# A graph attention layer: scores moved into PSUM, messages, queries and copies reordered

## The chip, the cores and the metric

The kernel runs on one core of one Trainium2 chip. The metric is device time in microseconds (us) of one execution. Five engines work from their own instruction queues: TensorE (PE; its weight loads are shown apart as PEld), VectorE (DVE), ScalarE (ACT), GpSimd (POOL) and SyncE (SP, which here only issues DMAs). An engine runs its instructions in program order, and semaphores order the engines among each other. So an instruction that waits holds up everything queued behind it on its engine. Line numbers (L630) are those of the kernel before; the profile shows one execution.

## The reference

One layer of a graph network: 6250 nodes with 64 channels, 4 heads of 16 channels, and 206250 directed edges sorted by their destination (each node has a loop on itself).

```python
Qh = (x @ Wq.T + bq).reshape(n, H, D)
Kh = (x @ Wk.T + bk).reshape(n, H, D)
Vh = (x @ Wv.T + bv).reshape(n, H, D)
Ee = (edge_attr @ We.T + be).reshape(-1, H, D)
score = (Kh[src] * Qh[dst] * (1.0 / np.sqrt(D)) * Ee).sum(-1)
score = jnp.exp(jnp.clip(score, -5.0, 5.0))
msg = Vh[src] * score[..., None]
wV = jax.ops.segment_sum(msg, dst, num_segments=n)
return layernorm(x + wV.reshape(n, H * D))
```

## The kernel before

A first stage (154 us, up to the first L600) computes k and v of every node into a table in HBM (`kv_tab`), the queries into another (`q3_tab`), and splits x into three bf16 parts (`parts`) that stay in SBUF. The rest is the loop over edges.

**Tiling.** The edges make 1612 tiles of 128 (an edge per partition). 8 tiles are a *group* (`g`, 202 of them), and an iteration of the main loop (L703) bears a group's number. Two groups are a *step* (`s`; the last 8 steps have one group). Four groups, two steps, are called a *round* here (`m = g // 4`, `i = g % 4` is the place in it).

**k and v of the sources.** They go into one of KVB = 5 buffers per step, a row per edge, in two ways. For 14 of the 16 tiles of a step GpSimd issues one indirect DMA per tile (`gather_kv`, L446; `gather(s)` issues a whole step's: first the 8 of the even group, then 6 of the odd one). A buffer is read by the messages of its step, so its refill waits for these: the 8 for the even group's message, the 6 for the odd group's. The other two tiles of a step are computed in 47 rounds, for the four tiles of two steps at a time. Their x rows are picked out of `parts` by products with one-hot matrices: VectorE compares (`hots`, L503, 13 a round in 7 buffers), TensorE multiplies (`picks`, L514 into bank `pick` and L519 into bank `low`, 100 matmuls a round). ScalarE copies the result into x2 and x1 (L526, L527). TensorE then multiplies by the k and v weights (`picked_kv`, a bias product at L530 and four products at L533 and L535, into `rooms`), and ScalarE copies the rows into the buffer (`place_kv`, L541).

**A group.** Its work, from iteration to iteration:

- `edges` (L435): the edge products, 8 fp32 matmuls into a `pe` bank (there are two, by turns), on top of a bias that ScalarE wrote there (`biases`, L564).
- `onehot_rows` (L571) and `onehot_rows_rest` (L577), ScalarE: a one-hot matrix `to` for each tile, which picks the row of each destination out of a window `qw` of 42 rows of the query table. `queries` (L594): 8 matmuls of `to` by `qw` into a `pq` bank (two, by turns), one iteration before each is used at the latest.
- `products` (VectorE): k times query (L600), times edge product (L601), sum over the 16 channels of a head (L604), clamp (L606).
- `weigh` (L610, ScalarE): the exponential, in place. `message` (L617, VectorE): v times the exponential into `msg`.
- per step: `onehot_edges` (L585, VectorE) and `widen` (L625, ScalarE) make a one-hot matrix of destinations, `sums` (L630, TensorE, 16 matmuls) adds the messages of equal destinations into `pa`, and `add` (L644, VectorE, two instructions) puts `pa` into the ring `acc`.
- when a block of 128 nodes is complete: `close`, `spreads`, `roots`, `scales`, `norm` (L658 to L683), the layer norm.

**Shared banks.** `pa` and `rooms` are two parts of one PSUM bank, `room`. Every reader and writer of one part is ordered against those of the other as the program stands: `picked_kv` behind the `add` that precedes it, `place_kv` behind the `sums` of its iteration, the next `add` behind `place_kv`.

**The order within an iteration** (L703 to L777) is written by hand, and each engine takes its own part of it. For iteration g before the change:

- VectorE: products(g), one hot, add of the step that ended at g-3, message(g-1), for odd g onehot_edges, the other hots of g+1, closes and norms.
- TensorE: picks of g, edges(g+1), for odd g-2 sums, queries(g+2), for even g picked_kv. (At i = 0 the picks come last.)
- ScalarE: the copies into x2 and x1 at i = 0, onehot_rows(g+4) and its rest, sources (the picks' comparands), widen, place_kv, biases(g+2), weigh(g).
- GpSimd: at the first group of step s, gather(s+4), whose 8 first DMAs wait for the message of the even group of step s-1 and whose 6 last for that of its odd group.
- SP: fetches of edge attributes, windows and keys, some groups ahead.

The `hots` of iteration g are compares for the picks of g+1. A hot waits until the picks (the low ones last) of the hot seven before it are done.

Of the kernel before, what the change touches and what calls it, by code (L numbers as in the profile page):

```python
# [7 lines left out]
F32 = mybir.dt.float32  # L8
# [6 lines left out]
P = 128  # L15
N = 6250
C = 64
H = 4
# [3 lines left out]
G = 8  # L22
NG = -(-T // G)

STEPS = [(g, 2) for g in range(0, NG - 8, 2)] + [(g, 1) for g in range(NG - 8, NG)]
NS = len(STEPS)
# [12 lines left out]
KVB = 5  # L39
# [9 lines left out]
def tiles_of(g):  # L49
    return min(G, T - g * G)  # L50


def tiles_in(s):
    return sum(tiles_of(g) for g in groups_of(s))


def groups_of(s):
    return range(STEPS[s][0], STEPS[s][0] + STEPS[s][1])
# [6 lines left out]
LAST = (NS - 8 - AHEAD) // 2  # L65
# [15 lines left out]
def is_picked(g, j):  # L81

    s = max(s for s in range(NS) if STEPS[s][0] <= g)
    return picks_in(s - AHEAD) and g == groups_of(s)[-1] and j >= G - 2
# [23 lines left out]
def tile_gnn(ctx: ExitStack, tc: tile.TileContext, x, xT, wT, bias, beT, weT, eT, src, src_rows, dst,  # L108
# [335 lines left out]
    def gather_kv(g, j):  # L444
        t = g * G + j
        nc.gpsimd.indirect_dma_start(  # L446
            out=kv_of(g)[:, j, :], out_offset=None, in_=kv_tab[:, :],
            in_offset=bass.IndirectOffsetOnAxis(ap=src_i[:, t:t + 1], axis=0))
# [8 lines left out]
    with tc.If(rv == 0) as branch:  # L457

        with tc.tile_pool(name="work", bufs=2) as work, \
# [3 lines left out]
            TO, OH, OF, PE, PQ, MSG, KB, SCORE, HOT, FROM, SRC = ({} for _ in range(11))  # L463
# [16 lines left out]
            def pairs(ap):  # L480

                return ap.rearrange("p (a b) -> p a b", b=2)
# [7 lines left out]
            def sources(m):  # L490
                if m < LAST:
                    FROM[m] = work.tile([P, BATCH * P], BF16, name="from")
                    nc.scalar.activation(FROM[m], SRC.pop(m), AF.Identity, bias=minus_row50)
# [5 lines left out]
            def hots(m, c):  # L499
                lo, hi = CUTS[c], CUTS[c + 1]  # L500
                HOT[m, c] = work.tile([P, MOST, BATCH * P], BF16, name="hot", bufs=7)
                shape = [P, hi - lo, BATCH * P // 2, 2]
                nc.vector.tensor_tensor(  # L503
                    HOT[m, c][:, :hi - lo].rearrange("p b (a c) -> p b a c", c=2),
                    pairs(FROM[m])[:, None].to_broadcast(shape),
                    block2[:, lo:hi, None, :].to_broadcast(shape), op=OP.is_equal)
# [31 lines left out]
            def place_kv(m, i):  # L538
                to = 2 * m + AHEAD + i
                n = tiles_in(to)  # L540
                nc.scalar.activation(kvs[to % KVB][:, n - 2:n, :], rooms, AF.Copy)  # L541

            def gather(s):

                for g in groups_of(s):
                    for j in range(tiles_of(g)):
                        if not is_picked(g, j):
                            gather_kv(g, j)
# [13 lines left out]
            def biases(g):  # L562
                n = tiles_of(g)
                nc.scalar.activation(pe_all[g % 2][:, :n, :],  # L564
                                     be_all[:, None, :].to_broadcast([P, n, C]), AF.Copy)
# [24 lines left out]
            def queries(g):  # L590
                PQ[g] = pq_all[g % 2]
                n = tiles_of(g)
                for j in range(n):
                    nc.tensor.matmul(PQ[g][:, j, :], TO[g][:, j, :], QW[g], start=j == 0,  # L594
                                     stop=j == n - 1, skip_group_check=True)

            def products(g):
                n = tiles_of(g)
                prod = work.tile([P, G, C], F32, name="prod")
                nc.vector.tensor_mul(prod[:, :n, :], kv_of(g)[:, :n, :C], PQ[g][:, :n, :])  # L600
                nc.vector.tensor_mul(prod[:, :n, :], prod[:, :n, :], PE[g][:, :n, :])  # L601
                SCORE[g] = work.tile([P, G, H], F32, name="score", bufs=3)
                score = SCORE[g][:, :n]
                nc.vector.tensor_reduce(score, prod[:, :n, :].rearrange("p g (h d) -> p g h d", h=H),  # L604
                                        axis=AX.X, op=OP.add)
                nc.vector.tensor_scalar(score, score, -5.0, 5.0, op0=OP.max, op1=OP.min)  # L606
# [5 lines left out]
            def message(g):  # L612
                s, k = place_of(g)
                if k == 0:
                    MSG[s] = work.tile([P, 2 * G, C], F32, name="msg")
                n = tiles_of(g)
                nc.vector.tensor_mul(MSG[s][:, k:k + n, :].rearrange("p g (h d) -> p g h d", h=H),  # L617
                                     kv_of(g)[:, :n, C:].rearrange("p g (h d) -> p g h d", h=H),
                                     SCORE[g][:, :n, :, None].to_broadcast([P, n, H, D]))

            def widen(s):

                n = tiles_in(s)
                OF[s] = work.tile([P, 2 * G, P], F32, name="off", bufs=1)
                nc.scalar.activation(OF[s][:, :n, :], OH.pop(s)[:, :n, :], AF.Copy)  # L625
# [61 lines left out]
            step_of = {g: s for s in range(NS) for g in groups_of(s)}  # L687
            ends = {groups_of(s)[-1]: s for s in range(NS)}
# [11 lines left out]
                queries(g)  # L700
            for mc in pieces(0):
                hots(*mc)
            for g in range(NG + 1):  # L703
                now, before = g < NG, g > 0
                i, m = g % 4, g // 4
                todo, ahead = pieces(g), pieces(g + 1)
                if g % LG == 0 and g + 2 * LG < NG:
                    fetch_edges(g // LG + 2)
                if i == 0 and m:
                    fetch_sources(m + 1)  # L710
                if g + 4 < NG:
                    fetch_queries(g + 4)
                if g + 6 < NG:
                    fetch_keys(g + 6)
                done = ends.get(g - 3)
                if now:
                    products(g)
                for mc in ahead[:1]:
                    hots(*mc)
                if done is not None:  # L720
                    add(done)
                if i == 0 and 0 < m <= LAST:
                    picked(m - 1)
                if i:
                    picks(todo)
                if 2 <= g + 1 < NG:
                    edges(g + 1)
                if g - 2 in ends:
                    sums(ends[g - 2])
                if g + 2 < NG:  # L730
                    queries(g + 2)
                if i in (0, 2) and 4 <= g <= 4 * LAST + 2:
                    picked_kv(i // 2)
                if i == 0:
                    picks(todo)
                if g + 4 < NG:
                    onehot_rows(g + 4)
                    onehot_rows_rest(g + 4)
                if i == 2 and g < 4 * LAST:
                    sources(m + 1)  # L740
                if g - 1 in ends:
                    widen(ends[g - 1])
                if i in (1, 3) and 4 <= g <= 4 * LAST + 3:
                    place_kv(m - 1, i // 2)
                if g + 2 < NG:
                    biases(g + 2)
                if now:
                    weigh(g)
                else:
                    add(NS - 2)  # L750
                if before:
                    message(g - 1)
                if now and g == groups_of(step_of[g])[0] and step_of[g] + KVB - 1 < NS:
                    gather(step_of[g] + KVB - 1)
                if g in ends:
                    s = ends[g]
                    t0 = STEPS[s][0] * G
                    for t in range(t0, t0 + tiles_in(s)):
                        if t and t % KEYS == 0:
                            keys(t)  # L760
                    onehot_edges(s)
                for mc in ahead[1:]:
                    hots(*mc)
                if done is not None:

                    while closed < B - 2 and due[closed] <= done + 1:
                        close(closed)
                        spreads(closed)
                        closed += 1
                    if closed in BATCHES and closed > scaled:  # L770
                        roots(scaled, closed)
                        scales(scaled, closed)
                        scaled = closed
                    for _ in range(3):
                        if normed < scaled:
                            norm(normed)
                            normed += 1  # L777
# [182 lines left out]
```

## Time and profile before

| | |
|---|---|
| runs | 2503.68, 2481.4, 2481.17 us |
| median of these | 2481.4 us |
| the profiled execution's own time | 2496.53 us |
| its span, first to last instruction | 2494.6 us |
| mean granted TensorE clock | 0.825 |
| TensorE busy (12299 matmuls) | 1935.9 us, 78% |
| TensorE weight loads | 1331.1 us, 53% |
| VectorE busy | 1494.2 us, 60% |
| GpSimd busy | 1350.8 us, 54% |
| ScalarE busy | 908.6 us, 36% |
| DMA, mean over the span | 92 GB/s |

All durations in the text come from the profiled execution. In a row of the profile's groups, the first pair of numbers is the busy time of all the group's instructions (us) and the mean of one (ns); behind the next bar stand the idle time of the engine just before them and what ended most of it. "issue" is time in which the engine waited for nothing that the profile shows, "remote" a release whose instruction it can't name. In the timeline a row is the start (us), the duration, the engine, line and instruction, "xN" for N in a row, and in brackets the idle time before it. In the windows a row is a stretch, its length, and the busy time of each engine in it with the number of its instructions; then the clock that TensorE was granted (1.00 is full), the share of time that the DMA engines were busy, and what they moved.

The first L600 starts at 154.0 us and the last at 2473.1; between them lie some 50 rounds; all 40 slices of the page between start and end look alike (TensorE busy 70 to 80%, clock 0.7 to 0.8), so the time is a matter of the round.

### The profile page before, as it was taken

The page shows a single profiled execution, that of the slowest core. Times are in us where ns is not written, and L with a number is a line of the kernel's source. Part 1 is how long each engine was busy: PE and PEld are TensorE (multiplying, and loading weights), DVE is VectorE, ACT ScalarE, POOL GpSimd, SP SyncE. Part 2 cuts the span into 40 slices and gives each one's busy share as a digit, 9 for nine tenths or more (in the row PEclk, how much of TensorE's full clock was granted, in tenths as well). Part 3 has the DMA queues.
Part 4 walks back from the last instruction along what each step waited for, and adds up shares of the span by engine and source line. Part 5 has one row for each costly group of instructions (what it writes and reads, how often), then busy time and mean ns, then how long its engine had stood idle before and what let it go on. Part 6 is the DMA issues. An engine that isn't in the chain of part 4 may idle for free. (4 is left out here: it accounts for less than half of the span.)

```text
span 2494.6 us, 32642 instructions
## 1 busy us (share of the span) xinstructions
PE 1935.9 (78%) x12299; PEld 1331.1 (53%) x12299; DVE 1494.2 (60%) x2314; ACT 908.6 (36%) x1268; POOL 1350.8 (54%) x1434
## 2 busy tenths in 40 slices
PE   4477887887887887877778788788788778788875
PEld 4435555555555555455555555555555555455574
DVE  2356665665666666666556566566666666666653
ACT  1242433433442434233424234233343343342452
POOL 5435555555555555555555555555555555555551
PEclk9978888887887888788788788788888788888865
DMA  4332333333332333333323233233333332332341
GB/s 119 125 96 77 100 91 86 99 97 82 99 97 80 98 91 104 87 83 97 95 82 92 79 101 98 78 99 90 91 103 86 88 101 79 95 93 83 87 114 25
DMA packets 140877, 228.84 MB, mean 92 GB/s; under 512 B 71126, under 2 KB 71576, under 8 KB 140598
## 3 DMA queue, kind: packets, MB, share of 16 engines
q1 hardware_dynamic: 94758, 133.30, 18.3%
q0 software_dynamic: 45568, 92.37, 14.2%
q8 instruction: 98, 1.61, 0.3%
q10 hardware_dynamic: 384, 1.00, 0.2%
q14 instruction: 69, 0.57, 0.1%
HBM read 218.74 MB, written 7.79 MB: 91 GB/s over the span
## 5 line engine op out<-in xcount | busy, mean ns | idle before, releaser
L446 POOL DMA_INDIRECT kv<-kv_tab,src_i x1392 | 1319.3, 948 | 1086.1 <-DVE msg L617 642.3
L503 DVE TENSOR_TENSOR hot<-from,still 128x2048 bf16<-128x2048 bf16 (+1 forms) x611 | 697.2, 1173 | 156.9 <-PE low L519 117.0
L630 PE MATMUL room<-msg,off 128*128 128x64 f32 x3224 | 498.3, 298 | 284.8 <-issue 277.4
L630 PEld LDWEIGHTS room<-msg,off 128*128 128x128 f32 x3224 | 472.9, 220 | 304.3 <-issue 296.0
L514 PE MATMUL pick<-hot,parts 128*128 128x512 bf16 x2350 | 583.8, 401 | 9.3 <-issue 9.0
L541 ACT ACTIVATE kv<-room 128x256 f32<-128x256 f32 x94 | 36.2, 385 | 1379.0 <-PE room L630 511.8
L514 PEld LDWEIGHTS <-parts 128*128 128x128 bf16 x2350 | 235.7, 103 | 299.1 <-issue 88.7
L601 DVE TENSOR_TENSOR prod<-prod,pe 128x512 f32<-128x512 f32 x202 | 138.8, 687 | 418.4 <-remote 323.7
L435 PE MATMUL pe<-we_sb,et 128*128 128x128 f32 x1612 | 292.0, 331 | 110.5 <-ACT pe L564 68.9
L435 PEld LDWEIGHTS pe<-we_sb,et 128*128 128x128 f32 x1612 | 243.3, 229 | 182.7 <-ACT pe L564 88.9
L519 PE MATMUL low<-hot,parts 128*64 128x512 bf16 x2350 | 306.1, 386 | 14.5 <-issue 13.8
L577 ACT ACTIVATE to<-to,one_p 126x1024 bf16<-126x1024 bf16 x202 | 232.0, 1148 | 6.6
L571 ACT ACTIVATE to<-kb,minus_row 126x1024 bf16<-126x1024 bf16 x202 | 230.0, 1139 | 10.9 <-remote 5.5
L519 PEld LDWEIGHTS <-parts 128*64 128x64 bf16 x2350 | 120.3, 110 | 190.0 <-issue 114.8
L625 ACT ACTIVATE off<-of 128x2048 f32<-128x2048 bf16 (+2 forms) x105 | 191.9, 1828 | 52.5 <-remote 20.8
L644 DVE SCALAR_TENSOR_TENSOR acc<-room,above,acc 128x64 f32<-128x64 f32 x103 | 29.0, 282 | 243.2 <-ACT kv L541 177.9
L600 DVE TENSOR_TENSOR prod<-kv,pq 128x512 f32<-128x512 f32 x202 | 137.5, 681 | 25.2 <-remote 6.8
L594 PE MATMUL pq<-qw,to 126*128 126x64 bf16 x1612 | 109.7, 217 | 50.4 <-issue 40.2
L617 DVE TENSOR_TENSOR msg<-kv,score 128x512 f32<-128x512 f32 x202 | 138.7, 687 | 16.9 <-ACT score L610 12.7
L604 DVE TENSOR_REDUCE score<-prod 128x32 f32<-128x512 f32 x202 | 138.3, 685 | 6.9
L594 PEld LDWEIGHTS <-to 126*128 126x128 bf16 x1612 | 103.4, 120 | 61.1 <-issue 56.5
L585 DVE TENSOR_TENSOR of<-still,key 128x2048 bf16<-128x2048 bf16 (+2 forms) x105 | 123.3, 1175 | 0.2
(122 smaller groups left out, 1050.1 us busy)
## 6 DMA issues: line engine op xcount, KB each, us to landing
et<-in_eT SPq DMA_DIRECT2D x100, 512.0 KB
kb<-key_tab SPq DMA_DIRECT2D x201, 252.0 KB
kv<-kv_tab,src_i POOLq DMA_INDIRECT x1392
srcs<-in_src_rows SPq DMA_DIRECT2D x47, 256.0 KB
qw<-q_tab SPq DMA_DIRECT2D x202, 15.8 KB
kv_tab<-kv_sb SPq DMA_DIRECT2D x5, 640.0 KB
q_tab<-q SPq DMA_DIRECT2D x5, 480.0 KB
acc<-in_x SPq DMA_DIRECT2D x48, 32.0 KB
```

The source lines that it names most:

```text
L435: nc.tensor.matmul(pe[:, 2 * u:2 * u + 2, :], et[:, u, :], we_sb, start=False, stop=u == n // 2 - 1, skip_group_check=True)
L446: nc.gpsimd.indirect_dma_start(out=kv_of(g)[:, j, :], out_offset=None, in_=kv_tab[:, :], in_offset=bass.IndirectOffsetOnAxis(ap=src_i[:, t ...
L503: nc.vector.tensor_tensor(HOT[m, c][:, :hi - lo].rearrange("p b (a c) -> p b a c", c=2), pairs(FROM[m])[:, None].to_broadcast(shape), bloc ...
L514: nc.tensor.matmul(hi_mid, parts_flat[:, at:at + 2 * C], hot, start=b == 0, stop=b == NB - 1)
L519: nc.tensor.matmul(low[u * C:(u + 1) * C], parts_flat[:, at:at + C], hot, start=b < 2, stop=b >= NB - 2, skip_group_check=True)
L571: nc.scalar.activation(TO[g][:, :n, :], KB.pop(g)[:, :n * P].rearrange("p (j e) -> p j e", j=n), AF.Square, bias=minus_row3[:3 * W])
L577: nc.scalar.activation(TO[g][:, :n, :], TO[g][:, :n, :], AF.Relu, bias=one_p[:3 * W], scale=-1.0)
L594: nc.tensor.matmul(PQ[g][:, j, :], TO[g][:, j, :], QW[g], start=j == 0, stop=j == n - 1, skip_group_check=True)
L601: nc.vector.tensor_mul(prod[:, :n, :], prod[:, :n, :], PE[g][:, :n, :])
L617: nc.vector.tensor_mul(MSG[s][:, k:k + n, :].rearrange("p g (h d) -> p g h d", h=H), kv_of(g)[:, :n, C:].rearrange("p g (h d) -> p g h d", ...
L625: nc.scalar.activation(OF[s][:, :n, :], OH.pop(s)[:, :n, :], AF.Copy)
L630: nc.tensor.matmul(pa, OF[s][:, j, :], MSG[s][:, j, :], start=j == 0, stop=j == n - 1)
```

## The change

Four edits in the kernel's loop.

- **Scores.** `SCORE[g]` is no longer a tile of its own in SBUF, but the first 32 floats of the group's own `pq` bank (the queries, which L601 has not read, but L600 has, by the time L604 writes). L604, L606, L610 and L617 then work on PSUM, and the next queries into that bank, those of g+2, come behind the message of g.
- **Message.** message(g) stands at the end of iteration g, behind onehot_edges and the hots; it was in iteration g+1, behind the first hot and the add.
- **Queries.** Iteration g issues queries(g+1); it was queries(g+2). The first two are issued ahead of the loop as before.
- **ScalarE.** The order is now onehot_rows, weigh, biases, widen, sources, place_kv.

And the gathers: with KVB = 5, gather(4) is issued ahead of the loop, and gather(s+5) at the end of step s, behind its last message; it was gather(s+4) at the first group of step s. The order of the gathers and what each waits for are unchanged.

```diff
@@ products
-                SCORE[g] = work.tile([P, G, H], F32, name="score", bufs=3)
+                SCORE[g] = PQ[g][:, 0, :G * H].rearrange("p (g h) -> p g h", h=H)
@@ before the loop
+            gather(KVB - 1)
             for g in range(NG + 1):
@@ in the loop
                     edges(g + 1)
                 if g - 2 in ends:
                     sums(ends[g - 2])
-                if g + 2 < NG:
-                    queries(g + 2)
+                if 2 <= g + 1 < NG:
+                    queries(g + 1)
                 if i in (0, 2) and 4 <= g <= 4 * LAST + 2:
                     picked_kv(i // 2)
...
                 if g + 4 < NG:
                     onehot_rows(g + 4)
                     onehot_rows_rest(g + 4)
-                if i == 2 and g < 4 * LAST:
-                    sources(m + 1)
-                if g - 1 in ends:
-                    widen(ends[g - 1])
-                if i in (1, 3) and 4 <= g <= 4 * LAST + 3:
-                    place_kv(m - 1, i // 2)
-                if g + 2 < NG:
-                    biases(g + 2)
                 if now:
                     weigh(g)
                 else:
                     add(NS - 2)
-                if before:
-                    message(g - 1)
-                if now and g == groups_of(step_of[g])[0] and step_of[g] + KVB - 1 < NS:
-                    gather(step_of[g] + KVB - 1)
+                if g + 2 < NG:
+                    biases(g + 2)
+                if g - 1 in ends:
+                    widen(ends[g - 1])
+                if i == 2 and g < 4 * LAST:
+                    sources(m + 1)
+                if i in (1, 3) and 4 <= g <= 4 * LAST + 3:
+                    place_kv(m - 1, i // 2)
                 if g in ends:
...
                     onehot_edges(s)
                 for mc in ahead[1:]:
                     hots(*mc)
+                if now:
+                    message(g)
+                if g in ends and ends[g] + KVB < NS:
+                    gather(ends[g] + KVB)
                 if done is not None:
```

More of the change, by code (lines that the diff above doesn't have):

```diff
@@ L702, in tile_gnn @@
                 hots(*mc)
+            gather(KVB - 1)
             for g in range(NG + 1):
-                now, before = g < NG, g > 0
+                now = g < NG
                 i, m = g % 4, g // 4
```

## The prediction

> **What bounds the kernel now.** I read the page first: engine table, slices, chain, groups. TensorE is the busiest engine (78%), but its idle time is not spread evenly, and the chain of waits names only the last microseconds. So the groups come next, for what ends idle time:
>
> ```profile
> L446 POOL DMA_INDIRECT kv<-kv_tab,src_i x1392 | 1319.3, 948 | 1086.1 <-DVE msg L617 642.3
> L630 PE MATMUL room<-msg,off 128*128 128x64 f32 x3224 | 498.3, 298 | 284.8 <-issue 277.4
> L541 ACT ACTIVATE kv<-room 128x256 f32<-128x256 f32 x94 | 36.2, 385 | 1379.0 <-PE room L630 511.8
> L601 DVE TENSOR_TENSOR prod<-prod,pe 128x512 f32<-128x512 f32 x202 | 138.8, 687 | 418.4 <-remote 323.7
> L435 PE MATMUL pe<-we_sb,et 128*128 128x128 f32 x1612 | 292.0, 331 | 110.5 <-ACT pe L564 68.9
> L644 DVE SCALAR_TENSOR_TENSOR acc<-room,above,acc 128x64 f32<-128x64 f32 x103 | 29.0, 282 | 243.2 <-ACT kv L541 177.9
> ```
>
> Two readings. The sums (L630) lose 285 us to "issue", waiting for nobody. And VectorE's L601 waits 324 us for a release that the profile cannot name. Third, the timeline of one half of a round of four groups (a round lasts 46.4 us on average, 47 of them pick rows):
>
> ```profile
> 928.53 0.62 PE L519 MATMUL low<-hot,parts 128*64 128x512 bf16 x4 [0.34 <-issue]
> 928.57 0.39 ACT L541 ACTIVATE kv<-room 128x256 f32<-128x256 f32 x1 [15.12 <-remote]
> 928.99 0.28 DVE L644 SCALAR_TENSOR_TENSOR acc<-room,above,acc 128x64 f32<-128x64 f32 x1 [5.16 <-ACT kv L541]
> 929.62 0.69 DVE L617 TENSOR_TENSOR msg<-kv,score 128x512 f32<-128x512 f32 x1 [0.16 <-ACT score L610]
> 930.58 0.94 POOL L446 DMA_INDIRECT kv<-kv_tab,src_i  x1 [3.63 <-DVE msg L617]
> 930.83 0.28 PE L530 MATMUL room<-bkv_p,ones_b 3*128 3x256 bf16 x1
> 936.13 1.16 PE L435 MATMUL pe<-we_sb,et 128*128 128x128 f32 x8
> 937.12 1.51 PE L630 MATMUL room<-msg,off 128*128 128x64 f32 x12
> 939.14 0.32 PE L630 MATMUL room<-msg,off 128*128 128x64 f32 x1 [0.51 <-issue]
> 946.84 0.94 POOL L446 DMA_INDIRECT kv<-kv_tab,src_i  x1 [0.30 <-issue]
> 950.39 1.75 PE L630 MATMUL room<-msg,off 128*128 128x64 f32 x7 [0.44 <-issue]
> 950.46 0.69 DVE L601 TENSOR_TENSOR prod<-prod,pe 128x512 f32<-128x512 f32 x1 [8.30 <-remote]
> ```
>
> L601 at 950.46 needs the edge products L435, which ended at 937.3: TensorE's signal reached VectorE 13 us late. Meanwhile TensorE issued about one matmul per 0.7 us. Both end 2.6 us after GpSimd finished a run of 14 gathers, one each 1.25 us (930.58 to 947.78). Counted over the trace, gathers under 0.6 us apart form 53 runs of 8, 48 of 6 and 45 of 14. In all three lengths TensorE's signals, good up to about 3 us into a run, mostly wait for its end: the first one after it comes 1.3, 1.6 and 2.6 us later (medians). Of 428 us that TensorE idles between 180 and 2330 us, 317 lie between 8 us after the start of a run of 14 and 2.7 us after its end; 6's and 8's have 91 in all. That is an inference from timing, not a mechanism I can see. The windows of the same stretch:
>
> ```profile
> core 0: us, PE busy (x) PEld busy (x) DVE busy (x) ACT busy (x) POOL busy (x), PEclk, DMA share, GB/s
> 930.60:939.00 8.40, 8.03 (x62) 5.23 (x59) 8.04 (x13) 6.43 (x8) 6.57 (x7) 1.00 0.69 182
> 939.00:950.40 11.40, 3.92 (x14) 3.12 (x14) 3.15 (x4) 0.00 (x0) 6.65 (x8) 0.61 0.17 46
> ```
>
> TensorE goes from 8.03 busy of 8.40 to 3.92 of 11.40, and its granted clock falls to 0.61, while DMA is nearly idle: no bandwidth limit. (The Trainium skill, "TensorE: Matmul & The Clock Gate", HAM clock gate, says an idle window of about 3.4 us halves the clock; the clock column agrees, and by that rule the waits of 1.3 and 2.0 us priced below would not add half-clock time of their own.)
>
> So: TensorE paces a round, and each gather run both blocks its signals and, if long, starves it. What matters of the change is which TensorE signals VectorE needs when, and how messages (which release gathers) cluster.
>
> **The change, part by part.**
>
> *Scores in the PSUM bank.* Same instructions. L600 reads one PSUM operand (681 ns), L601 too (687), L617 none (687): under 10 ns for PSUM, so 0, with ±0.01 x 3 x 202 = 6 us. (The Trainium skill, "Perfetto Trace Analysis", Identifying Performance Opportunities, gives VectorE about 60 ns of access overhead on SBUF, 125 on PSUM. By that, an estimate, 65 ns x 3 x 202 = 39 us if nothing hides it; no row here shows it, and VectorE idles 40%.) What the bank costs is order: queries of g+2 now wait for the message of g.
>
> *Queries one iteration later.* The same 8 weight loads and matmuls per group, now of g+1. Products of g+1 follow at once, so VectorE loses its lead: today it waits at L601 for the edge products, ahead of the sums; now at L600 for the queries, which follow the sums. ScalarE's one-hot rows also wait for the later queries, still 2.3 us ahead of the exponential's need. Put in times: an even iteration will start with the signal of the queries, which stand right behind the sums on TensorE. Where both were held back and land together, that is when L541 starts today (928.57, plus 0.1); where the sums ended by themselves (the first group of a round), the queries end 0.4 after L541 starts (904.33 + 0.64 = 904.97 against 904.57). Then products 2.35 (L600 0.79, L601 to the next hots 1.54), hots 1.2, and both adds 0.5 plus a gap: done 4.2 us after. The bias product of the picked rows (L530) needs these adds (they read the same bank). Today it starts 930.83 - 928.57 = 2.3 us after L541 in the third group of a round and 907.93 - 904.57 = 3.4 in the first. It will be 4.3 and 4.7: +2.0 and +1.3, 3.3 us of TensorE per round, 47 x 3.3 = **+155**. Lower bound 0: TensorE would have idled anyway in the following run. Upper bound: none of it hidden, which is what I take, as L530's successors wait behind it in order. What was queued behind on TensorE: all picks of the next group.
>
> *Copies of picked rows last on ScalarE.* Removes the wait of biases (L564) and exponential behind L541, hence of L435 for L564: 68.9 us + 3.8 for L625. This gain is already inside the +1.3 and +2.0, because today's 3.4 contains it. Widening is behind the exponential now: 1.9 us, done some 5 us after the products, while the next sums are a group away: 0; without that cover, 1.9 per step. The adds of the next even group wait for L541 as before.
>
> *Message in its own iteration, gathers after it.* Queue behind a waiting message on VectorE: closes, norms and the next products. The exponential is ready 0.3 us after the clamp and three hots (2.4 us or more) lie between, so L617 does not wait, save in the last 14 groups without hots: 14 x 0.5 = +7 (0 to 1.0 each; today's 12.7 us in all at L617 is the nearest row). On GpSimd the order stays 8 gathers on the even message, 6 on the odd one; step 4's gathers before the loop wait for nothing either way; SP's order is untouched. The timing is not: messages are now 12.7, 8.1, 16.0 and 10.2 us apart (0 to 1, 1 to 2, 2 to 3, 3 to 0), so one pair per round merges into 14. In the new order even message to odd message is one odd iteration: 2.35 + 1.2 + 1.2 (L585) + 2.4 to 2.9 + 0.7, plus up to 1.4 of closing and norms: 8 to 10 us, and 8 gathers take 10.0. So 8 + 6 may merge in both halves of a round, unless the odd iteration is held by a signal caught in the 8's run (the hots of the second group wait for the low picks of the first, about 3.5 us into it, where about half get through). Today's rounds in which one more run of 14 falls (1275, 1656, 1845, 1940, 2227 us) last with their follower 99.7, 96.0, 95.3, 95.8 and 98.3 us against 92.8 for two plain ones: +4.2 each. I take 4 in 10 rounds: 47 x 0.4 x 4.2 = **+79** (0 to +592, below).
>
> *Sum.* The profiled execution took 2496.5 us (span 2494.6); the median of the runs is 2481.4, 0.994 of it. 2496.5 + 155 + 79 + 7 = 2738, times 0.994 = **2720**.
>
> **Rivals.**
> 1. *Both halves merge.* Half a round is then: message at 7.1, first gather 7.4 after the queries' signal, run 17.2, lag 2.6, the rest of the sums and the queries 2.3 = 29.5, so 59 a round, +12.6 x 47 = +592: about 3070. For it: the 8 to 10 us above. Against: each caught signal separates the runs.
> 2. *Faster: no run of 14 is left.* Place: between even and odd message; it decides once these are over 10.0 + 1.6 = 11.6 us apart in both halves. Price: the 317 us go, the 155 + 7 stay: 2496.5 - 155 = 2341, times 0.994 = 2330. For it: today's merging pair (odd to even, 8.1 us) is pulled apart, and the low-pick wait holds the odd iteration. Against: the last half has no such wait.
> 3. *No change:* the added 3.3 us only fill time in which TensorE would stand in a gather run: 2480.
>
> **How the numbers follow.** Forecast 0.5 (2560 to 2850 by its own bounds), rival 1 0.2, rival 2 0.2, rival 3 0.1. Two in ten are left out by cutting off most of rival 2 and the upper half of rival 1: 2410 to 2980. About 1% is what a measurement here can tell. Faster: rival 2's 0.2 and 0.02 of rival 3; same: 0.06 of rival 3; slower: the rest, 0.72.
>
> **What would show it.** Right: L600 becomes VectorE's main wait in place of L601; L530 waits for L644; L435 no longer waits for L564; runs of 14 gathers per round rise from 0.95 towards 1.4; L630's "issue" idle stays or grows. Wrong: L630's issue idle well under 285 us with few runs of 14 (rival 2); two per round (rival 1); L530 without waits (rival 3); L617 or L606 well over 687 and 184 ns (the bank). If TensorE's late signals do not follow gather runs in the new trace, the whole of the second term falls.

## The result, and the profile after

| | before | after |
|---|---|---|
| median | 2484.1 us (4 runs) | 2951.1 us (4 runs) |
| lowest, highest | 2481.2, 2503.7 | 2944.6, 2957.4 |
| profiled execution | 2496.5 | 2957.4 |
| TensorE busy, clock | 1935.9 us, 0.825 | 2099.9 us, 0.758 |
| VectorE busy | 1494.2 us | 1489.9 us |
| GpSimd busy | 1350.8 us | 1348.7 us |

The ratio is 1.187, 95% interval 1.183 to 1.191: 467 us slower. TensorE runs the same 12299 matmuls and is busy 164 us longer, at a lower granted clock (0.758 against 0.825); the rest is idle time. Groups of the kernel after (in this kernel the numbers up to L701 are those of before):

```profile
L446 POOL DMA_INDIRECT kv<-kv_tab,src_i x1392 | 1317.2, 946 | 1546.4 <-DVE msg L617 545.9
L630 PE MATMUL room<-msg,off 128*128 128x64 f32 x3224 | 566.6, 316 | 440.2 <-issue 415.5
L600 DVE TENSOR_TENSOR prod<-kv,pq 128x512 f32<-128x512 f32 x202 | 138.3, 685 | 1208.5 <-PE pq L594 921.7
L435 PE MATMUL pe<-we_sb,et 128*128 128x128 f32 x1612 | 294.8, 330 | 68.3 <-issue 58.4
L604 DVE TENSOR_REDUCE pq<-prod 128x32 f32<-128x512 f32 x202 | 140.1, 694 | 7.0
L601 DVE TENSOR_TENSOR prod<-prod,pe 128x512 f32<-128x512 f32 x202 | 138.4, 685 | 7.0
```

VectorE's wait has moved from L601 (418 us idle) to L600 (1209 us): for the queries now, no longer for the edge products. L630's "issue" idle went from 277 to 416 us. L435 no longer names L564. A new wait stands in the table of waits (the two engines, us in total, times, longest):

```profile
PE room L530 <- DVE acc L644: 102.7, 46, 6.9
```

One half of a round in the timeline:

```profile
1154.25 0.69 DVE L600 TENSOR_TENSOR prod<-kv,pq 128x512 f32<-128x512 f32 x1 [12.54 <-PE pq L594]
1160.31 0.68 DVE L617 TENSOR_TENSOR msg<-kv,pq 128x512 f32<-128x512 f32 x1
1161.26 0.95 POOL L446 DMA_INDIRECT kv<-kv_tab,src_i  x1 [12.07 <-DVE y L658]
1167.90 0.89 PE L630 MATMUL room<-msg,off 128*128 128x64 f32 x7
1170.43 0.68 DVE L617 TENSOR_TENSOR msg<-kv,pq 128x512 f32<-128x512 f32 x1
1177.63 0.95 POOL L446 DMA_INDIRECT kv<-kv_tab,src_i  x1 [0.30 <-issue]
1178.29 0.68 PE L630 MATMUL room<-msg,off 128*128 128x64 f32 x2 [1.14 <-issue]
1181.08 1.76 PE L630 MATMUL room<-msg,off 128*128 128x64 f32 x8 [1.13 <-issue]
1182.63 0.64 PE L594 MATMUL pq<-qw,to 126*128 126x64 bf16 x8
1183.31 0.69 DVE L600 TENSOR_TENSOR prod<-kv,pq 128x512 f32<-128x512 f32 x1 [12.20 <-PE pq L594]
```

The first L617 is the even group's message; it starts 8 gathers. The odd group's message comes 10.1 us later, when the eighth is just being issued, so its 6 follow without a break: a run of 14, 17.3 us. TensorE starts the sums at 1167.90, 6.6 us into the run, issues about one per 0.7 us from the eighth on, and is at speed again at 1181.08, 2.5 us after the run. The queries stand behind these sums, and VectorE's products behind the queries: it sits idle for 12.2 us. In windows, before the slow stretch and in it:

```profile
1161.30:1169.00 7.70, 7.49 (x58) 4.86 (x56) 7.21 (x15) 4.38 (x6) 5.87 (x7) 1.00 0.79 199
1169.00:1181.00 12.00, 4.37 (x17) 3.74 (x17) 2.11 (x3) 0.00 (x0) 7.38 (x8) 0.63 0.19 51
```

Over the trace (groups 8 to 180): even to odd message 9.8 and 8.6 us, odd to even 20.1 and 19.0, a round 57.4 us against 47.4 before. 9.9 us by 47 rounds is 467 us, the whole difference. There are 83 runs of 14 gathers; before there were 45.

### The profile page after: what moved, and what is told of

Read it like the earlier page. It is cut to its first block, busy times and chain, and to the rows that moved or that the text cites. A ratio compares the mean times of both kernels' runs of the same rounds, so it can differ in the third digit from the quotient of the medians.

```text
span 2955.5 us, 32646 instructions
## 1 busy us (share of the span) xinstructions
PE 2099.9 (71%) x12299; PEld 1417.0 (48%) x12299; DVE 1489.9 (50%) x2314; ACT 925.0 (31%) x1268; POOL 1348.7 (46%) x1434
## 3 DMA queue, kind: packets, MB, share of 16 engines
q0 software_dynamic: 45568, 92.37, 12.2%
## 4 chain that ended last, share of the span: by engine, by line
PE 53%; issue 18%; DVE 16%; another core or an unknown queue 11%; ACT 1%; DMA 1%; POOL 0%; DVEq 0%; SPq 0%; ACTq 0%
PE pick L514 17%; PE room L630 15%; PE low L519 7%; DVE hot L503 6%; PE pe L435 4%; PE room L533 2%; DVE pq L604 2%; DVE prod L601 2%; DVE prod L600 2%; PE pq L594 2%; PE room L535 2%; DVE acc L644 1%; DVE msg L617 1%; DVE of L585 1%
## 5 line engine op out<-in xcount | busy, mean ns | idle before, releaser
L630 PE MATMUL room<-msg,off 128*128 128x64 f32 x3224 | 566.6, 316 | 440.2 <-issue 415.5
L630 PEld LDWEIGHTS room<-msg,off 128*128 128x128 f32 x3224 | 527.4, 237 | 467.0 <-issue 455.0
L600 DVE TENSOR_TENSOR prod<-kv,pq 128x512 f32<-128x512 f32 x202 | 138.3, 685 | 1208.5 <-PE pq L594 921.7
L514 PE MATMUL pick<-hot,parts 128*128 128x512 bf16 x2350 | 677.5, 449 | 8.8 <-issue 8.5
L514 PEld LDWEIGHTS <-parts 128*128 128x128 bf16 x2350 | 261.1, 114 | 366.8 <-issue 208.1
L435 PE MATMUL pe<-we_sb,et 128*128 128x128 f32 x1612 | 294.8, 330 | 68.3 <-issue 58.4
L435 PEld LDWEIGHTS pe<-we_sb,et 128*128 128x128 f32 x1612 | 248.0, 229 | 146.9 <-issue 130.3
L519 PE MATMUL low<-hot,parts 128*64 128x512 bf16 x2350 | 292.4, 385 | 2.1 <-issue 2.0
L594 PE MATMUL pq<-qw,to 126*128 126x64 bf16 x1612 | 135.2, 226 | 150.1 <-issue 143.1
L519 PEld LDWEIGHTS <-parts 128*64 128x64 bf16 x2350 | 117.5, 110 | 168.3 <-issue 87.1
L594 PEld LDWEIGHTS <-to 126*128 126x128 bf16 x1612 | 117.7, 127 | 166.9 <-issue 163.4
L617 DVE TENSOR_TENSOR msg<-kv,pq 128x512 f32<-128x512 f32 x202 | 137.3, 680 | 31.8 <-PE room L630 14.6
L604 DVE TENSOR_REDUCE pq<-prod 128x32 f32<-128x512 f32 x202 | 140.1, 694 | 7.0
L601 DVE TENSOR_TENSOR prod<-prod,pe 128x512 f32<-128x512 f32 x202 | 138.4, 685 | 7.0
L564 ACT ACTIVATE pe<-be_all 128x512 f32<-128x512 f32 x200 | 118.9, 594 | 0.0
```

The lines of the kernel that those rows point to most:

```text
L435: nc.tensor.matmul(pe[:, 2 * u:2 * u + 2, :], et[:, u, :], we_sb, start=False, stop=u == n // 2 - 1, skip_group_check=True)
L514: nc.tensor.matmul(hi_mid, parts_flat[:, at:at + 2 * C], hot, start=b == 0, stop=b == NB - 1)
L519: nc.tensor.matmul(low[u * C:(u + 1) * C], parts_flat[:, at:at + C], hot, start=b < 2, stop=b >= NB - 2, skip_group_check=True)
L630: nc.tensor.matmul(pa, OF[s][:, j, :], MSG[s][:, j, :], start=j == 0, stop=j == n - 1)
```

## The experiments

Most are single runs, each beside the kernel before on its own chip; the two groups of runs of the changed kernel itself agree (2951 and 2953 us). The chips turned out to differ, and this is told first, since every number needs it: on one (here chip A, the first and third group of runs) the kernel before takes 1824 and 1833 us, on the other (chip B, the second group) 2488 us, about as in the result above. Expectations that name 2484 us were meant for a chip like B.

**Without gathers.** In both kernels `gather(s)` in the loop does nothing, and the first five steps' buffers are filled at the start; k and v of most edges are then other edges' rows.

```diff
-    for g in range(XG, 2 * KVB - 2):
+    for g in range(XG, 2 * KVB):
...
             def gather(s):
-                for g in groups_of(s):
-                    for j in range(tiles_of(g)):
-                        if not is_picked(g, j):
-                            gather_kv(g, j)
+                pass
```

The kernel after with this cut:

> The changed kernel without the gathers inside the loop: the five buffers are filled once at the start and then read as they are, so k and v of most edges are wrong and about 94% of the loop's indirect DMAs are missing. Theory A (the added 467 us come from gather runs that merged: 83 runs of 14 against 45): without gathers the stalls of TensorE go, and this kernel lands at 2000 to 2250 us, no more than 160 us above the kernel before with the same cut; L630's issue idle falls from 415 us to under 40. Theory B (the added time is the chain itself: queries behind the sums, products behind the queries, whatever GpSimd does): it stays about 19% above the kernel before with the same cut, 350 us or more.

The kernel before with it:

> The kernel before with the same cut (no gathers inside the loop). Theory A: 1950 to 2100 us, since the 428 us of TensorE's idle time in the loop and part of the low clock go with the gathers; both theories agree on this kernel, it is the base for the other one.

Chip A: 1941 us after, 1729 us before. Without a single gather in the loop, the new order costs 212 us (ratio 1.123): more than the 160 that theory A allowed, less than the 350 of theory B. (Both times lie below the ranges expected, which were for the slower kind of chip.) L630 has no issue idle in either. Of the 212 us, 119 are TensorE's busy time (1756.5 against 1637.5, clock 0.905 against 0.975) and 86 its idle time in the loop (121.3 against 35.8). The timeline of the kernel after without gathers shows where (its lines behind the cut are 4 lower: L640 is the add, L560 the biases):

```profile
1014.25 0.28 DVE L640 SCALAR_TENSOR_TENSOR acc<-room,above,acc 128x64 f32<-128x64 f32 x1
1014.44 0.28 DVE L640 SCALAR_TENSOR_TENSOR acc<-room,below,acc 128x64 f32<-128x64 f32 x1
1014.77 0.39 PE L530 MATMUL room<-bkv_p,ones_b 3*128 3x256 bf16 x1 [2.76 <-ACT pe L560]
```

L530 starts right behind the second add; the biases named as releaser had ended just before, too, but the weight load of the same matmul names the add. The windows around it:

```profile
1008.00:1011.90 3.90, 3.90 (x47) 3.87 (x46) 3.67 (x6) 1.30 (x4) 0.00 (x0) 1.00 0.02 4
1011.90:1014.80 2.90, 0.14 (x5) 0.03 (x1) 2.83 (x7) 2.87 (x6) 0.00 (x0) 0.93 0.62 198
1014.80:1022.20 7.40, 7.40 (x25) 3.70 (x25) 4.95 (x7) 4.66 (x5) 0.00 (x0) 0.57 0.33 104
1022.20:1030.00 7.80, 7.80 (x58) 4.45 (x57) 5.21 (x5) 0.00 (x0) 0.00 (x0) 1.00 0.00 0
```

One wait of 2.8 us per round, and then 7.4 us at a clock of 0.57: the wait is paid for twice. In each round it is the first group's L530 that waits (2.8 us in nearly all rounds); the third group's waits once, 1.6 us, because there the picks stand ahead of `picked_kv` on TensorE and the adds are done meanwhile.

**The changed kernel again**, on chip B:

> The changed kernel itself, on the chip of this group of runs. The chips differ: in the last group the kernel before took 1824 us instead of 2484. Theory A: the change costs two things, (1) TensorE waits at L530 for adds that come later, 212 us in the pair without gathers (1941 against 1729), whatever the chip; (2) gather runs merge, which costs only on a chip where TensorE is held up during gather runs. On a chip where the kernel before takes about 1824 us it gives 2000 to 2100 us, ratio 1.10 to 1.15; where that takes 2484 us, 2951 again, ratio 1.19. Theory B (a chain of 19% of the time, whatever the chip): ratio 1.19 on both, 2165 us on the first kind.

2953 against 2488 us, ratio 1.189 (1.177 to 1.201), with 83 runs of 14 again. On such a chip both theories expected this number, so it doesn't decide between them; the half that would, the changed kernel on chip A, was not run.

**The edits one at a time**, all on chip B (2488 us). Queries alone:

```diff
-                if g + 2 < NG:
-                    queries(g + 2)
+                if 2 <= g + 1 < NG:
+                    queries(g + 1)
```

> The kernel before with the one edit that iteration g issues queries(g+1) instead of queries(g+2). Theory A: this edit carries the first part of the cost, since VectorE's products then wait for queries that stand behind the sums, and the adds come later: 60 to 100% of that part, ratio to the kernel before 1.07 to 1.14 on a chip where it takes 1824 us; L600 becomes VectorE's main wait and L530 waits for L644, 100 us or more. Rival (the cost lies in the message's or the copies' place): ratio below 1.03.

2793 us, +305 (1.122). The ratio is inside theory A's range, though that was given for the other kind of chip, and the rival's (below 1.03) is out. L600 became VectorE's main wait (1080 us idle, 842 for L594), as expected. L530 waits for L644 63.8 us, less than the 100 expected: ScalarE's old order holds L435 for L564 (73.3 us) beside it. The runs of 14 did not become more (46, against 45). So this edit alone costs two thirds of what the whole change costs here (465 us; the edits' costs don't add up, as the next one shows, so this is no share of it), and neither the count of merged runs nor the wait at L530 accounts for it. What did change: TensorE idles 154 us in runs of 8 (72 before), and the growth sits in one half of the round. From the first group's products to the third's it takes 26.7 us (25.9 before), from there to the next round's first 27.3 (21.6 before; means, groups 8 to 180). Before, VectorE waited at L601 for 6.9 us in the first group of a round and 0.7 in the third; now it waits at L600, behind the sums, for 11.7 and 10.3 us.

The message alone, with its gathers:

```diff
-                if before:
-                    message(g - 1)
...
+                if now:
+                    message(g)
+                if g in ends and ends[g] + KVB < NS:
+                    gather(ends[g] + KVB)
```

> The kernel before with the message of g at the end of iteration g and the gathers behind it, nothing else. Theory A: no wait is added for TensorE: within 2% of the kernel before on a chip where it takes 1824 us; on one where it takes 2484 us the gather runs merge (more than 60 runs of 14) and it costs 5 to 12%. Rival (the message's place is the first part's cost): ratio 1.07 or more on any chip.

3104 us, +616 (1.248), more than the whole change. The runs did merge (92 of 14), but the price was far over theory A's 5 to 12%. It is the rival's number (1.07 or more), seen on one kind of chip only, and the timeline has a reason that neither side had named:

```profile
1511.33 6.93 PE L630 MATMUL room<-msg,off 128*128 128x64 f32 x32
1518.30 0.38 ACT L541 ACTIVATE kv<-room 128x256 f32<-128x256 f32 x1 [21.66 <-PE room L630]
1519.10 0.22 ACT L610 ACTIVATE score<-score 128x32 f32<-128x32 f32 x1
1519.35 0.69 DVE L617 TENSOR_TENSOR msg<-kv,score 128x512 f32<-128x512 f32 x1 [14.55 <-ACT score L610]
```

In ScalarE's old order the copy of the picked rows waits for the sums, and the exponential stands behind the copy. A message in its own iteration needs that exponential at once: L617 waits 971 us for L610 in all. In the changed kernel, with ScalarE's new order, L617 waits 32 us.

The same trace says something about TensorE's slow stretches. The sums now mostly run ahead of a gather run, and the low picks (L519) stand in its late part. From the table of waits (the idle time before them that ends with no release):

```profile
PE low L519 <- issue: 300.7, 297, 2.4
PE room L630 <- issue: 46.0, 48, 1.9
```

Before, it was the other way round: 13.8 us at L519, 277.4 at L630. Of the 2761 sums that start outside gather runs and the 2.7 us behind them (and less than 3 us after the sum before), none starts over 0.45 us after the one before. So on chip B the slow stretch goes with the gather run, whatever TensorE issues in it.

ScalarE's order alone (weigh, biases, widen, sources, place_kv, as in the change's diff):

> The kernel before with ScalarE's new order alone (exponential, biases, widening, comparands, place_kv last). Theory A: the 55 to 69 us of L435's wait for L564 go and nothing comes in their place: ratio 0.97 to 1.00. Rival (the copies' late place makes the adds late, as L644 waits for L541): ratio 1.03 or more, L644's wait for L541 over 180 us.

2503 us, ratio 1.006, one run: no gain, but no such loss as the rival's (1.03 or more). L435's wait for L564 fell from 68.9 to 2.9 us as expected, and something came in its place all the same: L530 waits 36.8 us for L644, and L435's issue idle went from 36.7 to 79.4 us. Runs of 14 fell to 36.

**Message, gathers and ScalarE's order together**, queries and scores as before (the changed kernel with two edits undone):

```diff
-                SCORE[g] = PQ[g][:, 0, :G * H].rearrange("p (g h) -> p g h", h=H)
+                SCORE[g] = work.tile([P, G, H], F32, name="score", bufs=3)
...
-                if 2 <= g + 1 < NG:
-                    queries(g + 1)
+                if g + 2 < NG:
+                    queries(g + 2)
```

> The kernel before with message, gathers and ScalarE's order of the changed kernel together, queries (g+2) and scores (SBUF) as before. Theory A on a chip where the kernel before takes 2484 us: ScalarE's order takes away what made the message's place alone so dear (b_msg, 1.247: the message waits 971 us for the exponential behind the copies), no adds come late; but even and odd message come 8 to 11 us apart, so that 60 or more runs of 14 are left: ratio 1.02 to 1.10. On a chip where it takes 1824 us: 0.98 to 1.03. Rival (the queries' place is the only cost of the change): ratio 0.98 to 1.01 on both.

Chip A: 1828 us against 1833, ratio 0.998, which theory A and the rival both allowed. That doesn't show that these parts cost TensorE nothing: GpSimd paces this kernel (below), so a longer path on TensorE would stay hidden until it reaches 1828 us, 99 us over the 1729 of the kernel before without gathers. What follows is a bound. If the kernel doesn't get slower without its gathers, at least 1941 - 1828 = 113 of the 212 us belong to the queries' place and the scores together; the rest can be either's. For chip B it was not tried. Its trace shows something else, which changed the theory:

```profile
1008.13 0.95 POOL L446 DMA_INDIRECT kv<-kv_tab,src_i  x1 [0.30 <-issue]
1009.39 0.95 POOL L446 DMA_INDIRECT kv<-kv_tab,src_i  x1 [0.30 <-issue]
1009.44 3.68 PE L630 MATMUL room<-msg,off 128*128 128x64 f32 x32
1010.64 1.11 POOL L446 DMA_INDIRECT kv<-kv_tab,src_i  x1 [0.30 <-issue]
1012.06 0.94 POOL L446 DMA_INDIRECT kv<-kv_tab,src_i  x1 [0.30 <-DMA kv<-kv_tab,src_i]
```

GpSimd issues one run of 1348 gathers here, nearly the whole loop, each 1.25 us or so after the last, and a whole step's sums (two matmuls in the profile for each of its 16 tiles) pass through it in 3.68 us. Of L630's starts less than 3 us apart, 0.06% are over 0.45 us apart; in the kernels before and after on the slower kind of chip it is 12.5 and 17.4%. So gathers by themselves don't hold TensorE up. On a chip like B, something comes with them that does.

**Runs of gathers pulled apart.** Six `iota` instructions of 128x512 on GpSimd, in the kernel after between the 8 gathers and the 6, in the kernel before ahead of each step's 8:

```diff
             def gather(s):
                 for g in groups_of(s):
+                    if g != groups_of(s)[0] and len(groups_of(s)) == 2:   # before: g == groups_of(s)[0]
+                        for _ in range(6):
+                            nc.gpsimd.iota(idle, pattern=[[0, 512]], base=0, channel_multiplier=0)
```

> The changed kernel with six fillers of GpSimd (iota of 128x512, some 3 us in all) between the 8 gathers of an even group and the 6 of the odd group. Theory A: each run of 14 is broken into 8 and 6, TensorE's signals get through in the gap, few runs of 14 are left and the time falls to 2450 to 2700 us, although GpSimd does more. Theory B: nothing gained, 2950 us, or up to 300 us more where GpSimd's extra 3 us per step lie on the path.

> The kernel before with the same fillers, in front of each step's 8 gathers, which is where its runs of 14 join (the 6 of the odd group, then the 8 of the next step). Theory A: most of the 45 runs of 14 become 6 and 8, and the time falls to 2330 to 2430 us. Theory B: 2484 us or more.

2142 and 2148 us on chip A, both worse than the 1824 of the kernel before. There the stall that the fillers were to relieve does not exist, and they cost GpSimd: the 558 fillers take 557 ns each, one every 0.62 us, so that a step needs 14 x 1.25 + 6 x 0.62 = 21.2 us of GpSimd, and the traces show a median step of 21.4 and 21.0 us. So they test neither theory. Both kernels ran once more, with the changed kernel without gathers:

> The changed kernel with some 3 us of fillers on GpSimd between an even group's 8 gathers and the odd group's 6, once more. On a chip where the kernel before takes about 1824 us GpSimd paced it (2142 us, two steps' gathers joined). On one where it takes about 2484 us: theory A (merged gather runs hold up TensorE): 2450 to 2700 us against 2951, L630's issue idle under 300 us. Rival (the waits at L530 and L600 are all there is): 2950 us or more.

> The kernel before with the same fillers in front of each step's 8 gathers, once more. On a chip where the kernel before takes about 2484 us: theory A: fewer runs of 14 in one piece, 2330 to 2430 us, so faster than both kernels. Rival (TensorE is held up by gathers in any grouping): 2484 us or more.

> The changed kernel without gathers in the loop (k and v of most edges then wrong), once more. If the chips differ only in what gathers do to TensorE, it takes 1941 us within 2% on every chip. If the slower chip is slower by itself (clock, memory, instruction fetch), well over 2000 us on a chip where the kernel before takes 2484.

It was chip A again: 2142, 2151 and 1931 us, beside 1833 of the kernel before. These repeats only show how well such numbers hold (0.0, 0.1 and 0.5%).

**What this leaves.** Shown: the whole order costs 212 us without a gather in the loop (chip A); on chip B the queries' place alone costs 305 us and the whole change 465, and TensorE's slow stretches there go with gather runs. In the kernel after, 573 of the 721 us that TensorE idles in the loop lie between 8 us after the start of a run of 14 and 2.7 us after its end, which is 38% of that time. Not shown: that on chip B it is the gathers themselves that slow TensorE, since neither the pair without gathers nor the pulled-apart runs were tried there; and how the 465 us divide between the queries' place, the merged runs and the wait at L530. 467 - 212 = 255 us for the stalls is a difference between two chips, an estimate. No version beat both kernels: the nearest one is level with the kernel before on chip A, and there GpSimd paces it.

## Why the prediction was right or wrong

The direction and the range held (2410 to 2980); the forecast of 2720 had half of the loss (236 of 467 us). The measured 2951 lies outside the forecast's own bounds (2560 to 2850) and nearer to rival 1 (both halves merge, 3070), which had 0.2. The range holds it only because it took in the lower half of that rival, so this was in part luck.

- **The step that failed** is the second term: "I take 4 in 10 rounds: 47 x 0.4 x 4.2 = +79". Runs of 14 went from 45 to 83, 8 in 10 rounds, and a round grew by 9.9 us. The reason given against it, that the odd iteration may be "held by a signal caught in the 8's run", did not hold: even to odd message took 9.8 and 8.6 us, inside the 8 to 10 that the text had just worked out, and less than the 10.0 of 8 gathers. The iteration's own sum was to be trusted, not the discount on it. The price failed with the count: 38 more merged runs at 4.2 us are 160 us, and the whole sum would then have come to about 2800. What the traces show in its place is a round whose halves take 29.8 and 27.5 us where they took 25.9 and 21.6; with the queries alone moved they take 26.7 and 27.3, with no more merged runs. So the second half had grown as much without merging.
- **Rival 1's half** was right station by station. From one even product to the next: message at 7.1, first gather at 7.4, run of 17.2, 2.6 and 2.3 behind it, 29.5 in all. Measured medians: the message ends at 6.7, the first gather starts at 7.0, the run ends at 24.2, the next product starts at 29.7 and 27.2. The mean half is 28.7. Its price was too high by its base: 46.4 us is an average over all rounds, with the short ones at the end that pick no rows, and against the 47.4 us of a round that does, 59 is 11.6 us more, some 3020 us in all.
- **The first term (+155 at L530)** had the right wait in the wrong places and without its second price. The text had +2.0 us in the third group and +1.3 in the first; it is 1.6 to 3.7 us in the first (median 1.9) and, but for one round, none in the third, where the picks stand ahead of L530, 102.7 us in all. Without gathers the same wait is 2.8 us, and brings time at about half the clock with it; the pair differs by 212 us.
- **The clock.** The granted clock in the windows above falls to 0.57 after 2.8 us of idling. In the kernel after without gathers, the picks behind the 46 waits of 2.8 to 3.4 us at L530 are 0.43 us apart (median), against 0.216 where L530 didn't wait; behind the seven waits of 1.4 to 2.0 us in the trace with message, gathers and ScalarE's order moved, the median is 0.216. (The Trainium skill, "TensorE: Matmul & The Clock Gate", What's actually happening, has the clock halved after an idle window of about 3.4 us. Here less was enough, 2.8 us; by the rule the wait would have cost its own length alone.) Nor does the clock column of the prediction's windows agree with that rule, as its text has it: between 939 and 950.4 us TensorE was never idle for more than 1.2 us at a time, and its clock still fell to 0.61.
- **Scores in PSUM, 0:** right, as far as VectorE's own time goes. L600, L601, L604 and L617 take 554.1 us together, 553.3 before, and the clamp L606 takes 199 ns, 184 before. (The 39 us that the prediction worked out from the Trainium skill's "Perfetto Trace Analysis" are not there; the figures stand in its section Optimizing Scalar/DVE Operations.) The edit was not run alone.
- **Copies last:** L435's wait for L564 went (68.9 to 9.2 us), and by itself it gained nothing (b_act 1.006), as the sum had it. The cover named for the message held: L617 waits 32 us in all (17 before). With the message moved and ScalarE's old order (b_msg) it waited 971, a price that the text did not give.
- **What the sum had no term for** is the queries' place itself (305 us alone on chip B, with no more merged runs). It was treated as a matter of L530 and of merging. But sums stand in the odd iterations: before, an odd iteration's queries were for the next odd group, and an even group's had been issued one iteration earlier; now each even group's queries stand right behind sums, the last thing that TensorE issues in its slow stretch, and both halves of a round wait for them (12.2 us at L600 in the first group, 13.3 in the third, in the kernel after). Why the queries alone make the second half of the round 5.7 us longer and the first hardly at all stays open.
- **Rival 2** (no run of 14 left, 2330) and **rival 3** (2480) are out. The inference that TensorE's slow stretches follow gather runs holds in the new trace, and stays true where the message is moved alone, on the same chip; it falls as a rule for every chip: on chip A a run of 1348 gathers leaves the sums at full pace.

## What to carry to other kernels

Work that was issued one iteration ahead is a buffer against whatever makes an engine late: here, moving the queries from two groups ahead to one put them behind the slow sums and took 305 us by itself (chip B), although not one instruction was added. When an order gives two events a spacing that you can add up (8.6 to 9.8 us) and a transfer has a length (10.0 us), take the comparison as it stands instead of discounting it by hoped-for delays. And edits to an order belong together: the message's place alone cost more (616 us) than all four edits (465 us), and its trace shows why: in ScalarE's old order its exponential stands behind the copy that waits for the sums.

## What the runs showed of the hardware that was not expected

- The same kernel takes 1824 to 1833 us on one chip and 2472 to 2490 on another, with the same instructions. On the slower one TensorE issues fp32 sums about 0.7 us apart for long stretches, nearly all late in a run of gathers or just behind it, and its signals arrive late; with the message moved alone it is the low picks that stand there and lose the time (301 us at L519). On the faster one an unbroken run of 1348 gathers leaves the sums at 3.68 us for 32. The first stage, up to the first L600, takes 154 to 156 us on the slower kind of chip (76 gathers run in it) and 91 to 93 on the faster. What differs was not found.
- 2.8 us of idling of TensorE, once in a round of 37.5 us, was followed by 7.4 us at a granted clock of 0.57; and a stretch of 11.4 us without a single idle time over 1.2 us, but with TensorE busy for 3.9 us only, had 0.61.
